# Later slots for transfers, affine maps and softmax steps in a two-layer graph attention kernel

## Chip, cores and metric

The kernel runs on one core of one Trainium2 chip. The metric is the device time of one execution in microseconds; smaller is better. All arithmetic is in fp32.

## What is computed

The input is 128 graphs of 64 nodes with 768 features, and an adjacency matrix for each. After a layer norm with relu, two attention layers follow, and the result is added to the input:

```python
h = jnp.maximum(_layernorm(x, axis=-1), 0.0)
for l in range(2):
    m_left = jnp.einsum('bsh,oh->bso', h, W_left[l])
    m_right = jnp.einsum('bsh,oh->bso', h, W_right[l])
    u_left = jnp.einsum('bih,bjh->bij', h, m_left) / temper
    u_right = jnp.einsum('bih,bjh->bij', h, m_right) / temper
    u = u_left * adj_tri + u_left * diag_mask + u_right * jnp.swapaxes(adj_tri, 1, 2)
    delta_exp_u = jnp.exp(u) * adj
    attention = delta_exp_u / (jnp.sum(delta_exp_u, axis=2, keepdims=True) + 1e-10)
    h_lin = jnp.einsum('bsh,oh->bso', h, W_lin[l]) + b_lin[l]
    ctx = jnp.matmul(attention, h_lin)
    h = jax.nn.relu(_layer_norm(ctx, ln_a[l], ln_b[l]))
return x + h
```

## The kernel before

The 8192 tokens are cut into 16 blocks of 512 tokens (8 graphs each). A block stands in SBUF transposed, features on partitions, in one of four tiles `ht`. Each layer has two passes over all blocks, and DRAM holds what goes from one to the next.

**Pass one** (`pass_one`, L463) takes two blocks at a time; I call that a *set*, `U` = 0 to 7. `project` (L546) multiplies both blocks by the left (`k` = 0) and the right weights (`k` = 1). It does not form the 36 chunk products of 256 x 256 that this would take, but 29 products of sums of weight chunks with sums of token chunks (`PRODUCTS`, L129); each product's PSUM bank is then added, with a sign, to several chunks of the result tiles `m`, one tile per block, two tiles in all. For each of the 29 products and each `k` there are four matmuls (L559) into one PSUM bank, named X, Y, Z, V or aux, and then `read` (L307): the first time a chunk of `m` is written, ScalarE copies (L316); every later time, VectorE adds (L234). A first read happens only in products 0 to 11. Some products accumulate onto the bank of the product before them (product 3 onto product 2's), and then their matmuls wait for that bank's reads. The sums of token chunks (`X_OPS`, tiles `ts`) are made on GpSimd (also L234). The weight sums come from DRAM, where they were stored earlier, through a ring of eight tiles `wp` that is filled seven products ahead (`stream`, L210).

When a set's matmuls are done, `scores` (L488) multiplies `m` with the block's tokens: 192 matmuls of 32 x 95 for each block (L500), into the bank aux0. Before, both blocks' scores stand in one piece behind product 0 of the next set. Then comes the softmax of each block, a generator of eight steps (`chain`, L504): mask on GpSimd (L508), multiplication by the mask on VectorE (L514), exponential on ScalarE (L520), sums and division on VectorE, a transpose (L532), and eight stores of the attention (L537). Meanwhile the next two blocks are made ready: their rows are loaded (L381), in layer 0 normalised (L422, L426, L427), transposed on VectorE (L448), stored to DRAM in transposed form (L444) and loaded again as a block (L386). In layer 1 ScalarE then applies the layer norm's weights and the relu to the loaded block, six instructions called the *affine map* (L393).

The first set of layer 0 (`first`, L588) also normalises and turns its own two blocks on TensorE (`turn`, L648; statistics L635, copies L667), makes the weight sums on VectorE (negations on ScalarE, L199), and stores them (L207) for the later sets. Weight chunks there share tiles `ht2`, `ht3` and `wp` with what comes later. The two blocks themselves are stored, too (L704).

**Pass two** (`pass_two`, L826) multiplies each block by the linear weights in 15 products (`linear`, L1029; matmuls L1043, banks preset with the bias, L822), applies the attention (L851, L874) and normalises. During pass two of layer 0 the weight sums of layer 1 are made on GpSimd (`two_aside`, L1128: raw weights are loaded at L1133, then `weight_op`, then stored).

**What sets the order.** All transfers are issued by SP's queue, in the order of the program; one that has to wait holds those behind it. On every engine, instructions run in the order written. That order is written out with *slots*: in `project` each pair (product `i`, `k`) has two, after its first two matmuls and after its reads, so that a set has 116 slots, four for each product. `put(slot, f)` plans a piece of work for a slot, `put_all` a list of them at successive slots; `run` does what is planned for the slot, or else takes the next entry from the list `idle` (an entry `None` leaves a slot empty). In a set of layer 1, `block(n, slot)` at slots 14 and 62 plans, for the block, four transposes at every second slot, the store, the next rows and the load directly after them, the affine map eight slots on, and the softmax of an older block in eight successive slots.

## Time and profile before

| | |
|---|---|
| two runs | 2976.84 and 2993.67 us, median 2985.26 |
| profiled execution | 2991.47 us, of which the span from the first to the last instruction is 2989.7 |
| TensorE busy (matmul) | 2741.9 us, 92% of the span; mean granted clock 0.964 |
| VectorE / ScalarE / GpSimd busy | 1483.1 (50%) / 847.2 (28%) / 1333.4 us (45%) |
| DMA | 567.79 MB, mean 190 GB/s |
| stages | pass one of layer 0: 0 to 985 us; pass two: to 1488; pass one of layer 1: to 2489; pass two: to 2990 |

PE is TensorE, DVE is VectorE, ACT is ScalarE, POOL is GpSimd, SPq is SP's queue of transfers. A group such as `m<-m,aux` says what is written and read, by the names of tiles. The granted clock is the share of full speed that TensorE gets. In the waits, "A <- B: total, times, longest" says that A stood idle until B was done; "issue" means that nothing which the profile shows held it. A waiting instruction on one engine is often put down to an engine that itself waits, so a wait is followed back until something works.

### The profile page before, as it was taken

What the parts mean: (1) busy time and instruction counts of PE and PEld (TensorE: products, weight loads), DVE (VectorE), ACT (ScalarE), POOL (GpSimd) and SP (SyncE); (2) the same over time, 40 slices, a digit from 0 to 9 for tenths busy, and PEclk for the clock granted to TensorE, in tenths of its full rate; (3) what the DMA queues carried; (4) which work ended last, traced back from release to release, by engine and by line L of the source; (5) the groups of instructions that cost most, each with busy time, mean ns of one, the idle gap of its engine ahead of it and who ended that gap; (6) DMA issues with size and microseconds to landing.
All of it is one profiled execution on the core that took longest, in us unless ns stands there. A gap on an engine that the chain in (4) does not pass through costs nothing.

```text
span 2989.7 us, 47185 instructions
## 1 busy us (share of the span) xinstructions
PE 2741.9 (92%) x18514; PEld 2336.0 (78%) x18514; DVE 1483.1 (50%) x2469; ACT 847.2 (28%) x1635; POOL 1333.4 (45%) x1036
## 2 busy tenths in 40 slices
PE   7699999999999899999889889898898998999998
PEld 6588888888878788888678778787787877888886
DVE  5545546547447333333334434344353474666667
ACT  4221321321210144445521121211212111544443
POOL 3233333332435385655423234232342343888886
PEclk8899999999999999999999999899999999999999
DMA  7658668567673244455766766557675642555555
GB/s 260 188 191 274 207 191 269 186 216 247 193 259 131 98 160 153 159 174 163 223 215 193 230 199 224 175 189 218 196 236 180 213 151 71 149 170 170 164 173 141
DMA packets 310220, 567.79 MB, mean 190 GB/s; under 512 B 62832, under 2 KB 190064, under 8 KB 301808
## 3 DMA queue, kind: packets, MB, share of 16 engines
q1 hardware_dynamic: 309840, 564.39, 59.8%
q8 instruction: 148, 2.42, 0.3%
q14 instruction: 72, 0.59, 0.1%
q10 hardware_dynamic: 160, 0.39, 0.0%
HBM read 429.40 MB, written 135.27 MB: 189 GB/s over the span
## 4 chain that ended last, share of the span: by engine, by line
PE 75%; DMA 8%; DVE 5%; issue 3%; ACT 2%; SPq 2%; POOL 1%; DVEq 0%; ACTq 0%; POOLq 0%
PE aux L559 14%; PE X L1043 11%; PE Y L559 8%; PE X L559 8%; PE V L559 7%; PE V L1043 7%; PE Z L559 5%; PE Y L1043 5%; PE aux L500 4%; PE Z L1043 4%; DMA wp<-ws 3%; DMA ht<-h 2%; PE aux L851 2%; DVE m L234 2%; DMA room<-z 1%
## 5 line engine op out<-in xcount | busy, mean ns | idle before, releaser
L234 POOL TENSOR_TENSOR ts<-ht 128x512 f32<-128x512 f32 x352 | 476.5, 1359 | 294.1 <-PE aux L559 157.6
L234 POOL TENSOR_TENSOR ts<-ht,ht 128x512 f32<-128x512 f32 x128 | 164.6, 1296 | 936.2 <-PE aux L559 351.5
L559 PE MATMUL aux<-ts,wp 128*128 128x252 f32 (+1 forms) x1872 | 456.7, 389 | 123.0 <-DVE m L234 122.3
L559 PEld LDWEIGHTS aux<-ts,wp 128*128 128x128 f32 x1872 | 364.0, 196 | 181.2 <-DVE m L234 134.6
L234 POOL TENSOR_TENSOR ts<-ht,ts 128x512 f32<-128x512 f32 x192 | 254.4, 1329 | 166.7 <-PE aux L559 94.9
L234 DVE TENSOR_TENSOR m<-m,aux 128x504 f32<-128x504 f32 (+1 forms) x304 | 200.6, 673 | 247.0 <-ACT m L316 126.8
L234 DVE TENSOR_TENSOR m<-m,X 128x512 f32<-128x512 f32 x160 | 105.2, 682 | 400.5 <-ACT m L316 357.5
L1043 PE MATMUL X<-room,ts 128*128 128x256 f32 x1024 | 250.4, 387 | 17.6 <-POOL ts L234 7.5
L559 PE MATMUL Y<-ts,wp 128*128 128x256 f32 x1112 | 263.3, 380 | 1.0 <-DVE m L234 1.0
L1043 PEld LDWEIGHTS X<-room,ts 128*128 128x128 f32 x1024 | 195.0, 193 | 52.0 <-POOL ts L234 12.4
L559 PEld LDWEIGHTS Y<-ts,wp 128*128 128x128 f32 x1112 | 211.9, 191 | 29.6 <-issue 1.4
L393 ACT ACTIVATE ht<-ht,b_col,a_col 128x512 f32<-128x512 f32 x192 | 141.9, 803 | 248.5 <-DMA ht<-h 248.5
L500 PE MATMUL aux<-m,ht 128*32 128x95 f32 x6144 | 147.2, 256 | 45.2 <-issue 45.2
L1043 PE MATMUL Y<-room,ts 128*128 128x256 f32 x768 | 183.2, 380 | 0.0
L500 PEld LDWEIGHTS aux<-m,ht 128*32 128x32 f32 x6144 | 137.3, 116 | 56.6 <-issue 56.5
L234 DVE TENSOR_TENSOR m<-m,Y 128x512 f32<-128x512 f32 x176 | 118.2, 679 | 123.6 <-PE Y L559 108.1
L559 PE MATMUL Z<-ts,wp 128*128 128x256 f32 x736 | 174.3, 380 | 1.6 <-DMA wp<-ws 1.6
L1043 PEld LDWEIGHTS Y<-room,ts 128*128 128x128 f32 x768 | 146.7, 191 | 20.8 <-issue 0.6
L559 PEld LDWEIGHTS Z<-ts,wp 128*128 128x128 f32 x736 | 139.4, 190 | 21.5 <-DMA wp<-ws 3.1
L234 POOL TENSOR_TENSOR ts<-ts,ht 128x512 f32<-128x512 f32 x96 | 122.3, 1274 | 67.6 <-PE V L559 52.5
L234 DVE TENSOR_TENSOR hl<-hl,V 128x512 f32<-128x512 f32 (+1 forms) x136 | 88.9, 654 | 125.7 <-PE V L1043 113.6
L559 PE MATMUL X<-ts,wp 128*128 128x256 f32 x616 | 148.6, 385 | 0.0
(212 smaller groups left out, 4644.9 us busy)
## 6 DMA issues: line engine op xcount, KB each, us to landing
wp<-ws SPq DMA_DIRECT2D x435, 512.0 KB, 6.1
ht<-h SPq DMA_DIRECT2D x62, 1536.0 KB, 8.7
h<-room SPq DMA_DIRECT2D x112, 384.0 KB, 5.4
z<-z SPq DMA_DIRECT2D x128, 192.0 KB, 3.2
xr<-in_x_dram SPq DMA_DIRECT2D x120, 192.0 KB, 3.9
out_dram<-xr SPq DMA_DIRECT2D x120, 192.0 KB, 2.7
ws<-wp SPq DMA_DIRECT2D x84, 256.0 KB, 4.1
room<-in_x_dram SPq DMA_DIRECT2D x112, 192.0 KB, 5.3
```

The costliest lines, as they stand in the source:

```text
L234: (eng.tensor_add if sign == "+" else eng.tensor_sub)(o, a, b)
L393: nc.scalar.activation(ht, ht, AF.Relu, bias=cols[1][:, c:c + 1], scale=cols[0][:, c:c + 1])
L500: nc.tensor.matmul(p[h * S + e:h * S + e + 32, q, e:e + 95], ht[:, c, b * S + e:b * S + e + 32], mb[:, e:e + 95], start=(c == 0), stop=(c ...
L559: nc.tensor.matmul(p[:, g], wk[:, c, g * P:(g + 1) * P], tk[:, c, :].rearrange("p (b s) -> p b s", s=S)[:, :, :ns], start=(new and g == c ...
L851: nc.tensor.matmul(cx[k][i, m, :HH], at[j, q, :], hl[j, q, m * HH:(m + 1) * HH], start=True, stop=True)
L1043: nc.tensor.matmul(p[:, n], b[t][:, c, r * P:(r + 1) * P], w[s][:, c, :], start=(i in FIRST and i not in PRELOAD and n == c == 0), stop=(c ...
```

## The change

It moves work between slots; apart from which tiles hold the last block's adjacency and mask, what is computed and what is transferred stays the same.

- In pass one the two blocks' scores come apart: the first block's behind product 0 of the next set, the second's behind product 2. The second result tile `m` is taken anew behind product 2, and reads into it that are due before are held back.
- For each block, transposes start at slots 6 and 48 (layer 1; 20 and 48 in its first set), 6 and 56 (layer 0), 40 and 77 (first set of all). The store follows four slots after the last one, the next rows one later, the load of the block thirteen slots after the transposes, and the affine map 22 slots after the load.
- The softmax has slots of its own, 20 to 34 and 60 to 74, one step in every second slot.
- In each pass's last set both first blocks of pass two are loaded (slots 12 and 40) and mapped (38 and 66). The softmax of the very last block is run in slots 2 to 9 of pass two; its adjacency and mask are kept in a tile of the weight ring.
- In the first set, the turns of the last four row groups come at slots 8, 12, 19 and 24 instead of 9, 11, 17 and 19, the stores of the two first blocks at 54 and 58 instead of 13 and 21.
- In pass two of layer 0 empty slots are put behind the raw weights' loads and behind each weight operation.

The functions `prepare` and `both_scores` go, and the line numbers fall by 4 to 21: the affine map is L381, ScalarE's first read L304, the scores L483, the block load L374, the row loads L369, the block store L432, the first blocks' store L688, the attention's store L520, the stores of weight sums L195, the stream L198, project's matmuls L538, the exponential L503, and additions L222.

```diff
-    singles = [RING[i][:, n] for i in range(RINGS) for n in range(2)]
+    singles = [RING[(NU * NP + 1 + i) % RINGS][:, n] for i in range(RINGS) for n in range(2)]
...
+            def spare(n):
+                return RING[NU * NP % RINGS][:, n].rearrange("p c (q k s) -> p (c q) k s", k=2, s=S)
             def load_adj(u):
-                ADJ[u] = sp.tile([P, Q, 2, S], F32, name="adj")
+                ADJ[u] = spare(0) if u == NB - 1 else sp.tile([P, Q, 2, S], F32, name="adj")
...
-                    wm = sp.tile([P, Q, 2, S], F32, name="wm", bufs=2)
+                    wm = spare(1) if u == NB - 1 else sp.tile([P, Q, 2, S], F32, name="wm", bufs=2)
...
+            TURNS = {0: 0, 2: 1}
             def project(U, weights, done):
...
-                        if i == 0 and k == 1:
+                        late.append((k, p, ns, what))
+                        if k and i in TURNS:
                             if U:
-                                both_scores(U - 1)
-                            for n in range(2):
-                                M[2 * U + n] = sp.tile([P, C, NBB, 2, S], F32, name="m", bufs=2)
-                        for kk in range(2) if (i, k) == (0, 1) else (k,) if i else ():
-                            p, ns = state[kk]
+                                if i == 0:
+                                    both = aux(0)
+                                scores(2 * U - 2 + TURNS[i], both[:, TURNS[i]])
+                            M[2 * U + TURNS[i]] = sp.tile([P, C, NBB, 2, S], F32, name="m", bufs=2)
+                        now, late = late, []
+                        for kk, p, ns, what in now:
+                            if any(2 * U + int(o, 16) % 4 // 2 not in M for o in what[1::2]):
+                                late.append((kk, p, ns, what))
+                                continue
                             read(p, lambda o: M[2 * U + o % 4 // 2][:, o // 4 * K2:(o // 4 + 1) * K2,
...
-                for n, (s0, s1, s2, s3) in {4: (4, 5, 6, 9), 5: (6, 7, 8, 11), 6: (12, 13, 14, 17),
-                                            7: (14, 15, 16, 19)}.items():
+                for n, (s0, s1, s2, s3) in {4: (3, 4, 5, 8), 5: (6, 7, 8, 12), 6: (13, 14, 15, 19),
+                                            7: (17, 18, 20, 24)}.items():
...
-                for n, slot in ((0, 13), (1, 21)):
+                for n, slot in ((0, 54), (1, 58)):
                     put(slot, lambda n=n: nc.sync.dma_start(KEPT[0][n], hts[n]))
...
-                        todo = prepare(u)
-                        load = todo.pop(-2) if u + 1 < NB else todo.pop()
-                        slot = put_all(slot + 1, todo)
-                        slot = max(slot, (86, 99)[n]) if U == 0 and l == 0 else slot
-                        put(slot - 1, load)
+                        *todo, store = transpose_rows(l, u)
+                        slot = put_all(slot, todo)
+                        put(slot + 4, store)
+                        if u + 1 < NB:
+                            put(slot + 5, lambda: load_rows(l, u + 1))
+                        slot = max(slot + 13, (92, 107)[n]) if U == 0 and l == 0 else slot + 13
+                        put(slot, lambda: load_h(1, l, u))
                         if l:
-                            put_all(slot + 8, affine(1, l, u))
-                        if U:
-                            put_all(slot + 1, softmax(u - 4) + [lambda u=u: load_adj(u - 2)])
-
-                    for n, slot in enumerate((32, 60) if U == 0 and l == 0 else (14, 62)):
-                        put(slot, lambda n=n, slot=slot: block(n, slot))
+                            put_all(slot + 22, affine(1, l, u))
+
+                    if l:
+                        starts = (6 if U else 20, 48)
+                    else:
+                        starts = (6, 56) if U else (40, 77)
+                    for n, slot in enumerate(starts):
+                        put(slot - 1, lambda n=n, slot=slot: block(n, slot))
+                    if U:
+                        for n in range(2):
+                            put_all(20 + 40 * n, softmax(2 * U - 2 + n) + [lambda n=n: load_adj(2 * U + n)], 2)
                     put_token_ops(l, U + 1, "before")
                 else:
-                    put(12, lambda: load_h(2, l, 0))
-                    slot = put_all(30, affine(2, l, 0))
                     for n in range(2):
-                        put_all(14 + 10 * n, softmax(2 * U - 2 + n) + [lambda n=n: load_adj(2 * U + n)])
+                        put(12 + 28 * n, lambda n=n: load_h(2, l, n))
+                        put_all(38 + 28 * n, affine(2, l, n))
+                    for n in range(2):
+                        put_all(14 + 20 * n, softmax(2 * U - 2 + n), 2)
+                    put(32, lambda: load_adj(2 * U))
+                    put(SLOTS - 12, lambda: load_adj(2 * U + 1))
...
-            both_scores(NU - 1)
-            for a, b in zip(softmax(NB - 2), softmax(NB - 1)):
-                a()
-                b()
+            both = aux(0)
+            for n in range(2):
+                scores(NB - 2 + n, both[:, n])
+            for f in softmax(NB - 2):
+                f()
+            put_all(2, softmax(NB - 1))
...
-            if (2, l, 0) not in HT:
-                load_h(2, l, 0)
...
                 if u + 1 < NB:
-                    load_h(2, l, u + 1)
-                    put_all(9 if u else 15, affine(2, l, u + 1))
+                    if u:
+                        load_h(2, l, u + 1)
+                        put_all(9, affine(2, l, u + 1))
...
                 idle.extend([lambda n=n, kind=kind: raw(kind, n) for n in range(9)])
+                idle.extend(none * (12 if kind == "l" else 4))
                 for i in range(NP):
-                    ops = [op for op in W_OPS if op[0] == i]
-                    idle.extend([lambda op=op, kind=kind: weight_op(ss, kind, op, nc.gpsimd) for op in ops])
-                    idle.extend(none * min(len(ops), 1))
+                    for op in W_OPS:
+                        if op[0] == i:
+                            idle.extend([lambda op=op, kind=kind: weight_op(ss, kind, op, nc.gpsimd), None])
+                    if idle[-1] is None:
+                        idle.pop()
                     idle.append(lambda i=i, kind=kind: kept(kind, i))
```

What this does to the order, first on ScalarE in set 3 of layer 1, around products 10 and 11. `m_11643` and `m_11644` (now `m_11545` and `m_11675`) are the result tiles, `ht0` and `ht1` the blocks for the next set. Before:

```order
L316 ACTIVATE m_11643<-V_11706 128x2x4x63
L520 ACTIVATE adj_11101<-adj_11101 128x4x64
L316 ACTIVATE m_11643<-Y_11786 128x2x4x64
L393 ACTIVATE ht0_11746<-ht0_11746,b_col_604,a_col_602 128x512 x2
L316 ACTIVATE m_11643<-aux1_9535 128x2x4x63
L393 ACTIVATE ht0_11746<-ht0_11746,b_col_604,a_col_602 128x512 x4
L316 ACTIVATE m_11643<-X_11695 128x2x4x64
L316 ACTIVATE m_11644<-X_11695 128x2x4x64
L316 ACTIVATE m_11643<-V_11706 128x2x4x63
L316 ACTIVATE m_11644<-V_11706 128x2x4x63
```

After:

```order
L503 ACTIVATE adj_11106<-adj_11106 128x4x64
L304 ACTIVATE m_11545<-Y_11784 128x2x4x64
L304 ACTIVATE m_11545<-aux1_9533 128x2x4x63
L304 ACTIVATE m_11545<-X_11696 128x2x4x64
L304 ACTIVATE m_11675<-X_11696 128x2x4x64
L304 ACTIVATE m_11545<-V_11706 128x2x4x63
L304 ACTIVATE m_11675<-V_11706 128x2x4x63
L381 ACTIVATE ht0_11762<-ht0_11762,b_col_602,a_col_600 128x512 x6
L503 ACTIVATE adj_11305<-adj_11305 128x4x64
L381 ACTIVATE ht1_11969<-ht1_11969,b_col_602,a_col_600 128x512 x6
```

The map of the first block (`ht0`) stood between the first reads of products 10 and 11, and now stands behind the last of them.

Next, TensorE at the begin of the same set, with the scores of the set before (`aux0` is their bank). Before:

```order
L559 MATMUL Y_11441<-ht2_11034,wp7_84 128x256 x4
L559 MATMUL aux1_9535<-ht2_11034,wp7_84 128x252 x4
L500 MATMUL aux0_11450<-m_10931,ht0_10322 32x95 x96
L500 MATMUL aux0_11450<-m_10932,ht1_10550 32x95 x96
L559 MATMUL Z_11648<-ht3_11262,wp0_77 128x256 x4
L559 MATMUL aux1_9535<-ht3_11262,wp0_77 128x252 x4
L559 MATMUL X_11666<-ht2_11034,wp1_78 128x256 x4
L559 MATMUL V_11674<-ht2_11034,wp1_78 128x252 x4
L559 MATMUL X_11666<-ts10_11432,wp2_79 128x256 x4
```

After:

```order
L538 MATMUL Y_11439<-ht2_11050,wp7_84 128x256 x4
L538 MATMUL aux1_9533<-ht2_11050,wp7_84 128x252 x4
L483 MATMUL aux0_11448<-m_10833,ht0_10338 32x95 x96
L538 MATMUL Z_11549<-ht3_11257,wp0_77 128x256 x4
L538 MATMUL aux1_9533<-ht3_11257,wp0_77 128x252 x4
L538 MATMUL X_11564<-ht2_11050,wp1_78 128x256 x4
L538 MATMUL V_11573<-ht2_11050,wp1_78 128x252 x4
L483 MATMUL aux0_11448<-m_10963,ht1_10545 32x95 x96
L538 MATMUL X_11564<-ts10_11430,wp2_79 128x256 x4
L538 MATMUL V_11573<-ts10_11430,wp2_79 128x252 x4
```

Two products now stand between the halves of the scores. On ScalarE, the reads that follow, after:

```order
L304 ACTIVATE m_11545<-Y_11439 128x2x4x64
L304 ACTIVATE m_11545<-aux1_9533 128x2x4x63
L304 ACTIVATE m_11545<-X_11564 128x2x4x64
L304 ACTIVATE m_11675<-Z_11549 128x2x4x64 x2
L304 ACTIVATE m_11675<-aux1_9533 128x2x4x63 x2
L304 ACTIVATE m_11545<-V_11573 128x2x4x63
L304 ACTIVATE m_11675<-X_11564 128x2x4x64
L304 ACTIVATE m_11675<-V_11573 128x2x4x63
```

The four reads of Z and aux1 into `m_11675` stand ahead of the read of V from product 2; before, both result tiles were free from the scores on, which stood ahead of product 1.

Last, SP in the first set of layer 0; `ws0` are the stored weight sums by product, `h0_0` and `h0_1` the two first blocks. Before:

```order
L207 DMA ws0_2_88<-room_85 128x512 x2
L704 DMA h0_0_144<-ht0_315 128x3072
L207 DMA ws0_3_89<-ht3_247 128x512 x2
L207 DMA ws0_4_90<-wp7_84 128x512 x2
L704 DMA h0_1_145<-ht1_316 128x3072
L207 DMA ws0_5_91<-room_85 128x512 x2
L381 DMA room_85<-in_x_dram 32x2x768 x8
L207 DMA ws0_6_92<-wp2_79 128x512
L207 DMA ws0_6_92<-ht3_247 128x512
L322 DMA a_col_602<-in_ln_a_dram 128x6x1
L322 DMA b_col_604<-in_ln_b_dram 128x6x1
```

After:

```order
L195 DMA ws0_2_88<-room_85 128x512 x2
L195 DMA ws0_3_89<-ht3_247 128x512 x2
L195 DMA ws0_4_90<-wp7_84 128x512 x2
L195 DMA ws0_5_91<-room_85 128x512 x2
L369 DMA room_85<-in_x_dram 32x2x768 x8
L195 DMA ws0_6_92<-wp2_79 128x512
L195 DMA ws0_6_92<-ht3_247 128x512
L310 DMA a_col_600<-in_ln_a_dram 128x6x1
L310 DMA b_col_602<-in_ln_b_dram 128x6x1
```

The stores of the two first blocks no longer stand among those of the first six products' weight sums, and the row loads move up behind those. Further down the queue, after, the loads of blocks 2 and 3 (`ht2`, `ht3`):

```order
L195 DMA ws0_24_110<-wp4_81 128x512
L432 DMA h0_3_147<-room_85 192x4x128 x4
L369 DMA room_85<-in_x_dram 32x2x768 x8
L195 DMA ws0_25_111<-wp6_83 128x512
L195 DMA ws0_25_111<-wp2_79 128x512
L198 DMA wp5_82<-ws0_0_86 128x1024
L198 DMA wp6_83<-ws0_1_87 128x1024
L198 DMA wp7_84<-ws0_2_88 128x1024
L195 DMA ws0_26_112<-wp3_80 128x512
L195 DMA ws0_26_112<-wp1_78 128x512
L374 DMA ht3_1025<-h0_3_147 128x3072
```

Block 3's load comes behind the first three transfers of the weight stream (`wp5` to `wp7`); before, it stood ahead of them.

More of the change, by code (lines that the diff above doesn't have):

```diff
@@ L539, in scores @@
                 CHAIN[u] = chain()
[L541 to L544 removed]
+            TURNS = {0: 0, 2: 1}
             def project(U, weights, done):
[L547 removed]
+                bank, seen, late = {}, (set(), set()), []
                 for i, (w, t, at, new, what) in enumerate(PRODUCTS):
[L549 removed]
                     for k in range(2):
```

18 lines of the change are left out of this document (3 added, 15 removed).

## Prediction

> **What bounds the kernel now.** First the stages: columns are length, then busy time and instructions of TensorE, its weight loads, VectorE, ScalarE and GpSimd, the granted clock, the share of the DMA engines and GB/s. The rows are the first product set, one set of layer 0, one of layer 1.
>
> ```profile
> 0.00:172.14 172.14, 125.50 (x563) 106.23 (x563) 96.80 (x165) 52.27 (x98) 57.80 (x52) 0.89 0.73 236
> 517.25:632.98 115.73, 110.55 (x850) 97.14 (x849) 62.38 (x116) 27.16 (x40) 39.70 (x35) 0.99 0.68 220
> 1733.21:1860.51 127.30, 111.02 (x850) 97.05 (x849) 54.18 (x88) 22.77 (x38) 41.52 (x36) 0.95 0.63 201
> ```
>
> TensorE is the bound; no other compute engine is busy for even 60% of a set. So the change can only give back TensorE's idle and half-clock time. A set of layer 1 takes 11.6 us longer than one of layer 0 with the same matmuls. Next, TensorE's own waits (total, times, longest), asked stage by stage: three rows of the first set, two of the rest of layer 0's pass one, two of its pass two, one of layer 1's pass one without its last set, one with it, two of layer 1's pass two.
>
> ```profile
> PE aux L559 <- DVE m L234: 29.0, 4, 18.7
> PE aux L658 <- DVE ht L667: 5.1, 2, 4.2
> PE X L559 <- ACT ht L199: 5.0, 1, 5.0
> ...
> PE aux L500 <- issue: 28.0, 11, 3.9
> PE aux L559 <- DVE m L234: 8.9, 11, 2.6
> ...
> PE X L1043 <- ACT hl L316: 14.2, 2, 11.4
> PE X L1043 <- POOL ts L234: 7.5, 1, 7.5
> ...
> PE aux L559 <- DVE m L234: 92.7, 12, 13.7
> PE aux L500 <- issue: 14.6, 14, 3.4
> PE X L1043 <- ACT X L822: 4.1, 1, 4.1
> PE X L1043 <- ACT hl L316: 2.9, 1, 2.9
> ```
>
> The 92.7 us are the largest piece. The timeline of one of them shows who is really late:
>
> ```profile
> 1763.60 4.63 SPq L444 DMA_DIRECT2D h<-room  x4
> 1770.18 6.93 SPq L381 DMA_DIRECT2D room<-z  x8
> 1777.34 0.34 SPq L386 DMA_DIRECT2D ht<-h  x1
> 1779.79 9.69 SPq L537 DMA_DIRECT2D att<-wm  x8
> 1786.51 1.52 ACT L393 ACTIVATE ht<-ht,b_col,a_col 128x512 f32<-128x512 f32 x2 [16.93 <-DMA ht<-h]
> 1787.93 0.57 ACT L316 ACTIVATE m<-aux 128x504 f32<-128x504 f32 x1
> 1788.53 0.68 DVE L234 TENSOR_TENSOR m<-m,aux 128x504 f32<-128x504 f32 x1 [17.39 <-ACT m L316]
> 1789.27 3.31 PE L559 MATMUL aux<-ts,wp 128*128 128x252 f32 x7 [13.46 <-DVE m L234]
> ```
>
> Read upwards: TensorE waits for a PSUM bank, the bank for an addition, the addition for a first read (m<-aux) that stands on ScalarE behind the affine map of a block still in flight. The load left SP at 1777.34, behind eight row loads, and its data were there 9.2 us later. VectorE and ScalarE are victims; what stands ahead of what on ScalarE is the cause.
>
> **The change, term by term.** A slot is a quarter of a product. Products follow each other every 3.42 us (1746.50 to 1749.92 in a fence below), so a slot is 0.86 us.
>
> *A, affine maps.* Before, a layer-1 set's first block is stored at slot 23, loaded at 24 and mapped at 33 to 38, ahead of ScalarE's first reads of products 10 and 11 (slots 40 to 47). After: store 18, rows 19, load 27, map 49 to 54, behind the last first read. From load to map there are 22 slots instead of 9, 18.9 us. SP has the store (4.6 us), the rows (6.9) and some streams ahead of the load; that reaches about slot 34, and 9.2 us of flight end at slot 44. Were the load later still, ScalarE would next hold up the second softmax's exponential near slot 66, 22 slots on. So I take all seven long waits as gone: of the 92.7 us some 91, since five of the twelve are short. After each, TensorE runs for some us at half clock:
>
> ```profile
> 1789.27:1799.27 10.00, 10.00 (x38) 8.62 (x39) 4.27 (x7) 4.20 (x7) 3.77 (x3) 0.81 0.79 284
> ```
>
> 10 us at 0.81 lose 1.9 us, which I use for each long wait; times seven, 13. **A = 104** (bounds 83, if 3 us of each wait stay, to 110).
>
> *B, scores apart.* The 384 small matmuls of a set's scores now come as 192, two products, 192. Inside them TensorE waits for nothing but its own instructions, 28.0 + 14.6 us. The gaps are longer, and halve the clock, where transfers crowd (a set's begin in layer 0, then in layer 1):
>
> ```profile
> 639.23:649.23 10.00, 8.55 (x224) 8.00 (x224) 0.00 (x0) 1.20 (x3) 4.62 (x4) 0.83 0.37 152
> 1863.00:1873.00 10.00, 8.41 (x284) 7.58 (x276) 0.00 (x0) 1.42 (x3) 0.00 (x0) 1.00 0.06 22
> ```
>
> A set's scores meet about two gaps; if the instructions for the second half arrive during the 6.8 us of the products between, 192 meet one half of the time, one gap per set: half of 42.6 goes, 21. That they do is inferred, not shown. The softmax stores and the adjacency load leave the set's end, so the rest of layer 0's gaps should shrink towards layer 1's: 8 more, and 9 of the 7 x 1.7 us of half clock. Against it stands a new wait. Product 1 now has to wait for the second block's result tile, which is free only after the second scores; its four reads queue on ScalarE ahead of the read of product 2's bank V, into which product 3 accumulates.
>
> ```profile
> 1746.50 1.89 PE L559 MATMUL X<-ht,wp 128*128 128x256 f32 x8
> 1746.70 1.07 ACT L316 ACTIVATE m<-aux 128x504 f32<-128x504 f32 x2 [0.61 <-PE aux L559]
> 1749.92 1.89 PE L559 MATMUL X<-ts,wp 128*128 128x256 f32 x8
> 1750.12 0.59 ACT L316 ACTIVATE m<-V 128x504 f32<-128x504 f32 x1 [1.10 <-PE V L559]
> ```
>
> After the scores: 0.2 to start, two such pairs of 1.07, the read of V, 0.6, and a hand-over, about 3.0 us, against 1.7 us (half a product) of product 3's first matmuls: TensorE stands 1.3 us, in 14 sets 18 us. Behind the waiting V matmul stands all of TensorE's queue. **B = 21 + 8 + 9 - 18 = 20** (bounds -18, only the new wait, to 45).
>
> [...]
>
> *C, softmax steps every second slot instead of every slot.* TensorE's short waits for additions (8.9 in layer 0, about as much in layer 1, the largest in each pass's last set, whose weight sums stay) lose a third. **C = 5** (0 to 10).
>
> *D, first set.* Four long waits: 18.7, 7.5 (the second of the 29.0), 5.0, 4.2.
>
> ```profile
> 131.99 1.95 SPq L207 DMA_DIRECT2D ws<-ht  x2
> 139.24 0.32 SPq L386 DMA_DIRECT2D ht<-h  x1
> 149.64 1.29 DVE L234 TENSOR_TENSOR wp<-room,wp 128x512 f32<-128x512 f32 x2 [19.48 <-DMA ws<-wp]
> 61.57 0.69 DVE L234 TENSOR_TENSOR ht<-ht,wp 128x512 f32<-128x512 f32 x1 [8.31 <-DMA ws<-ht]
> 110.71 0.18 DVE L427 RECIPROCAL rs<-sd 128x4 f32<-128x4 f32 x1 [8.30 <-ACT sd L426]
> ```
>
> The longest: SP stood 5.3 us at the block load until weights in that tile were stored; the weight stores behind it went out late, and VectorE needed their tiles. Seven slots later most of that has landed. The 7.5: row loads held a weight store, and were late themselves behind the store of a first block that waited for its turn; that store now comes at slots 54 and 58. The 4.2 goes with four slots between two turns instead of two, the 5.0 with block 3's statistics at slot 77 instead of 61, behind the negations that TensorE wanted. With 4 x 1.9 that is 43. Two new waits: block 3's rows land about slot 84, behind the statistics that want them (up to 8.3 on VectorE, last row; I take 5), and block 3's load stands behind three streams that wait for product 25, issues near slot 119 and is wanted near 125, with ten slots of flight (I take 5). VectorE, busy 96.8, has less slack: 5. **D = 28** (10 to 43).
>
> *E, pass starts.* Before, both softmaxes run on VectorE ahead of pass two's first addition, and ScalarE's read behind two exponentials: 2.9 us per layer. Now one goes ahead, the other over slots 2 to 9.
>
> ```profile
> 994.54 4.51 DVE L514 TENSOR_TENSOR wm<-aux,wm 32x380 f32<-32x380 f32 x8 [8.45 <-issue]
> 1025.67 1.26 POOL L234 TENSOR_TENSOR wp<-wp 128x512 f32<-128x512 f32 x1 [40.24 <-DMA wp<-in_w_left_dram]
> ```
>
> The weight operations now stand behind GpSimd's token sums, so the 7.5 goes; block 1 is loaded and mapped within pass one, so layer 1's 4.1 goes. With 1.9 for each and less 1.5 per layer for the second softmax between the additions (about a third of the 4.51): layer 0 2.9 + 7.5 + 3.8 - 1.5, layer 1 2.9 + 4.1 + 3.8 - 1.5. **E = 22** (12 to 25). The 11.4 us at the turn of the layers stay; SP's order there is nearly the same.
>
> Sum: 104 + 20 + 5 + 28 + 22 = 179. The profiled execution took 2991.47 us (span 2989.7); less 179 that is 2812. It lay 6.2 above the median of the runs shown, so I forecast **2806 us**.
>
> **Rivals.** *The scores give nothing.* For it: gaps of 3.4 us also in layer 1, where transfers are few. Against: the longer ones come with the crowded transfers. B = -18, the sum 141: 2844.
>
> *The wait moves.* The load is late for its new slot as well, the map holds the exponential, that holds VectorE. For it: ScalarE waited 16.9 us for the load. Against: 22 slots of slack. With half of A left, 2858.
>
> *Transfers bind.* A set moves 127.3 us x 201 GB/s, 25.6 MB; at the 220 GB/s of layer 0 it could not pass below 116 us, where I count on 111: 7 x 5 back, 2841. Against: nothing shows 220 to be a ceiling; the first set ran at 236.
>
> *Slower.* SP takes everything in order, and eight ring tiles let the weight stream run seven products ahead: 7 x 3.42 = 23.9 us; with about 9 of flight, as for the load above, 15 are left. A block's transfers need 4.6 + 6.9 + 0.3 + 9.7 = 21.5 us of SP. If spread out they left the stream unserved for longer than 15, TensorE would stand for the excess at each of 28 blocks. The change is a loss from 21.4 us on (179 / 28 = 6.4 over), and at 24 us it ends at 2806 + 28 x 9 = 3058. For it: SP is held at more places in a set. Against: streams stand between the pieces in the new order, and the softmax stores, the longest piece, now come apart from the rows.
>
> *The change does nothing* would need the maps still ahead of the first reads; the order shows that they aren't.
>
> **How the numbers follow.** Forecast 0.70, no gain from the scores 0.11, transfers bind 0.07, the wait moves 0.07, slower 0.04, nothing 0.01. All lower bounds together make a sum of 87, 2898; all upper ones 233, 2752. They won't fall together, so I take 2765 to 2870, which holds the three milder rivals. Over 2% faster is below 2925.6, about what a measurement of this kernel can tell: the forecast and these three, less some for several at once, 0.91; within 2% 0.05; slower 0.04.
>
> **What would show it.** A: no idle ScalarE at the map before product 12, and sets of layer 1 at 110 to 113 us, as long as layer 0's. B: one gap per set's scores, and about 1.3 us before product 3's V matmul. D: no wait over 8 us in the first set. E: pass two of layer 0 without a wait for GpSimd. Wrong, if sets of layer 1 stay above 118 us, or TensorE waits for wp<-ws more than a few us in all.

## The result, and the profile after

The changed kernel takes **2829.85 us** (two runs, 2829.77 and 2829.93) against 2985.26 before: a ratio of 0.9479, 95% interval 0.9365 to 0.9594. The forecast was 2806, the range 2765 to 2870. The gain is 155 us where 179 were counted, and the table shows that most of the difference sits in one stage, the later sets of layer 0. A set runs here from the first matmul of its scores to that of the next, and pass two of layer 1 to the end of TensorE's last matmul; the two profiled executions are compared.

| stage | before, us | after, us | gained |
|---|---|---|---|
| first set of layer 0 | 172.1 | 149.2 | 23.0 |
| the seven sets behind it | 812.6 | 817.8 | -5.2 |
| pass two of layer 0 and first set of layer 1 | 624.5 | 592.6 | 31.9 |
| the seven sets behind it | 880.0 | 778.5 | 101.5 |
| pass two of layer 1 | 489.4 | 479.1 | 10.4 |

Another execution of the changed kernel (e9 below) has 812.8 in place of 817.8, so the -5.2 is known to some 5 us: layer 0's later sets gained nothing.

The stage view (columns as in the prediction's first fence), of the changed kernel: first set, the same sets of layer 0 and layer 1 as before.

```profile
0.00:149.16 149.16, 124.85 (x563) 106.10 (x563) 100.12 (x174) 52.66 (x98) 43.86 (x40) 0.92 0.77 255
504.78:620.74 115.96, 111.15 (x849) 96.79 (x848) 64.21 (x116) 26.90 (x40) 39.54 (x34) 0.99 0.67 221
1668.49:1779.02 110.53, 108.48 (x850) 95.65 (x849) 55.15 (x89) 22.46 (x38) 40.45 (x34) 1.00 0.72 231
```

Layer 1's set fell from 127.3 to 110.5 us at a full clock, and is now shorter than layer 0's, which did not move. TensorE's waits, first over the span (the head of the answer), then the additions alone, asked for layer 0's later sets and for those of layer 1 without its last:

```profile
PE aux L538 <- DVE m L222: 23.1, 18, 3.2
PE aux L483 <- issue: 20.1, 16, 2.6
PE X L1039 <- ACT hl L304: 11.5, 3, 9.3
PE Y L538 <- DMA wp<-ws: 8.9, 5, 4.2
PE V L538 <- ACT m L304: 8.7, 12, 0.7
PE X L538 <- ACT ht L187: 7.4, 1, 7.4
```

```profile
PE aux L538 <- DVE m L222: 16.8, 13, 2.4
```

```profile
PE aux L538 <- DVE m L222: 0.3, 1, 0.3
```

The 92.7 us for additions in layer 1 are 0.3. In layer 0 the same wait grew, from 8.9 to 16.8. The timeline of one such wait (in the set of layer 0 above), VectorE's rows and then the row of TensorE that waits:

```profile
538.87 0.98 DVE L436 STREAM_TRANSPOSE room<-room 128x768 f32<-128x768 f32 x1
539.77 0.38 DVE L501 TENSOR_TENSOR adj<-wm 128x256 f32<-128x256 f32 x1
540.08 1.83 DVE L436 STREAM_TRANSPOSE room<-room 128x768 f32<-128x768 f32 x2
541.94 0.69 DVE L222 TENSOR_TENSOR m<-m,Z 128x512 f32<-128x512 f32 x1
542.54 0.42 DVE L505 TENSOR_TENSOR adj<-adj 128x256 f32<-128x256 f32 x1
542.99 0.42 DVE L507 TENSOR_REDUCE s<-adj 128x4 f32<-128x256 f32 x1
543.33 0.97 DVE L436 STREAM_TRANSPOSE room<-room 128x768 f32<-128x768 f32 x1
544.22 0.64 DVE L222 TENSOR_TENSOR m<-m,aux 128x504 f32<-128x504 f32 x1
```

```profile
544.92 1.63 PE L538 MATMUL aux<-ht,wp 128*128 128x252 f32 x3 [2.38 <-DVE m L222]
```

VectorE does softmax (L501 to L507) and block transposes (L436) in turn, without a pause, and the addition that empties TensorE's bank comes behind them. In layer 0 a block starts at slot 6 with its statistics and normalisation, so the transposes fall on slots 24 to 30; the softmax was put at 20 to 34. All six sets from the second to the seventh have this wait, 2.25 to 2.39 us long.

The 8.9 us for `wp<-ws`, the weight stream, are 4.2 at the end of the first set and 4.7 in layer 0's later sets, where the kernel before had 0.9.

Next, the load and the map of a layer-1 set (it starts at 1668.49): SP's queue, then ScalarE.

```profile
1693.78 0.37 SPq L374 DMA_DIRECT2D ht<-h  x1
```

```profile
1717.33 1.07 ACT L304 ACTIVATE m<-V 128x504 f32<-128x504 f32 x2 [0.61 <-PE V L538]
1718.28 4.33 ACT L381 ACTIVATE ht<-ht,b_col,a_col 128x512 f32<-128x512 f32 x6
```

The map follows the last first read without a wait, as forecast. But the load leaves 25.3 us after the set's start, where before it left after 44.1 (1777.34 - 1733.21): much earlier than the slot 34 that the prediction counted for it, which comes 37.5 us after the set's start.

### The profile page after: what moved, and what is told of

Read it like the earlier page. It is cut to its first block, busy times and chain, and to the rows that moved or that the text cites. A ratio compares the mean times of both kernels' runs of the same rounds, so it can differ in the third digit from the quotient of the medians.

```text
span 2827.8 us, 47204 instructions
## 1 busy us (share of the span) xinstructions
PE 2720.0 (96%) x18514; PEld 2315.8 (82%) x18514; DVE 1500.9 (53%) x2469; ACT 843.5 (30%) x1635; POOL 1337.4 (47%) x1036
## 3 DMA queue, kind: packets, MB, share of 16 engines
q8 instruction: 148, 2.42, 0.4%
## 4 chain that ended last, share of the span: by engine, by line
PE 77%; DVE 8%; DMA 4%; ACT 4%; SPq 3%; issue 3%; POOL 2%; DVEq 0%; ACTq 0%; POOLq 0%
PE aux L538 14%; PE X L1039 11%; PE Y L538 8%; PE V L1039 8%; PE X L538 7%; PE V L538 7%; PE Y L1039 6%; PE Z L538 5%; PE aux L483 4%; PE Z L1039 4%; DVE m L222 3%; ACT m L304 2%; DMA wp<-ws 2%; PE aux L847 2%; DVE room L436 2%
## 5 line engine op out<-in xcount | busy, mean ns | idle before, releaser
L222 POOL TENSOR_TENSOR ts<-ht 128x512 f32<-128x512 f32 x352 | 479.3, 1367 | 313.9 <-PE aux L538 203.9
L222 POOL TENSOR_TENSOR ts<-ht,ht 128x512 f32<-128x512 f32 x128 | 163.9, 1286 | 713.5 <-PE aux L538 288.1
L538 PE MATMUL aux<-ts,wp 128*128 128x252 f32 (+1 forms) x1872 | 439.9, 378 | 7.2 <-DVE m L222 7.2
L538 PEld LDWEIGHTS aux<-ts,wp 128*128 128x128 f32 x1872 | 356.2, 191 | 55.7 <-DVE m L222 11.2
L222 POOL TENSOR_TENSOR ts<-ht,ts 128x512 f32<-128x512 f32 x192 | 254.5, 1329 | 173.3 <-PE aux L538 81.2
L222 DVE TENSOR_TENSOR m<-m,aux 128x504 f32<-128x504 f32 (+1 forms) x304 | 200.9, 674 | 153.8 <-PE aux L538 132.4
L538 PE MATMUL Y<-ts,wp 128*128 128x256 f32 x1112 | 265.9, 382 | 5.8 <-DMA wp<-ws 4.7
L1039 PE MATMUL X<-room,ts 128*128 128x256 f32 x1024 | 244.2, 380 | 2.3 <-ACT hl L304 2.2
L538 PEld LDWEIGHTS Y<-ts,wp 128*128 128x128 f32 x1112 | 212.1, 191 | 36.9 <-issue 6.0
L222 DVE TENSOR_TENSOR m<-m,X 128x512 f32<-128x512 f32 x160 | 105.0, 681 | 233.8 <-ACT m L304 189.7
L222 DVE TENSOR_TENSOR m<-m,Y 128x512 f32<-128x512 f32 x176 | 119.0, 684 | 141.4 <-PE Y L538 137.2
L304 ACT ACTIVATE m<-Y 128x512 f32<-128x512 f32 x32 | 19.1, 597 | 564.6 <-PE aux L483 523.1
L222 POOL TENSOR_TENSOR ts<-ts,ht 128x512 f32<-128x512 f32 x96 | 123.1, 1282 | 113.8 <-PE V L538 71.0
L538 PE MATMUL Z<-ts,wp 128*128 128x256 f32 x736 | 174.0, 379 | 0.0
L381 ACT ACTIVATE ht<-ht,b_col,a_col 128x512 f32<-128x512 f32 x192 | 141.1, 804 | 107.6 <-DMA ht<-h 107.6
L483 PE MATMUL aux<-m,ht 128*32 128x95 f32 x6144 | 137.8, 246 | 20.1 <-issue 20.1
L538 PEld LDWEIGHTS Z<-ts,wp 128*128 128x128 f32 x736 | 139.7, 190 | 19.1 <-POOL ts L222 0.3
L1005 POOL TENSOR_TENSOR z<-z,b 128x768 f32<-128x768 f32 x62 | 112.7, 1831 | 89.8 <-DVE z L1002 89.8
L538 PE MATMUL V<-ts,wp 128*128 128x252 f32 (+1 forms) x608 | 143.8, 379 | 11.7 <-ACT m L304 8.7
```

The source lines that it names most:

```text
L222: (eng.tensor_add if sign == "+" else eng.tensor_sub)(o, a, b)
L304: nc.scalar.activation(to(o), p, AF.Copy, scale=1.0 if sign == "+" else -1.0)
L381: nc.scalar.activation(ht, ht, AF.Relu, bias=cols[1][:, c:c + 1], scale=cols[0][:, c:c + 1])
L483: nc.tensor.matmul(p[h * S + e:h * S + e + 32, q, e:e + 95], ht[:, c, b * S + e:b * S + e + 32], mb[:, e:e + 95], start=(c == 0), stop=(c ...
L538: nc.tensor.matmul(p[:, g], wk[:, c, g * P:(g + 1) * P], tk[:, c, :].rearrange("p (b s) -> p b s", s=S)[:, :, :ns], start=(new and g == c ...
L1005: nc.gpsimd.tensor_add(zs[k], zs[k], rows["b"])
```

## Experiments

e1 to e4 ran on one chip, e5 to e8 on a second, e9 to e12 on a third. The kernel before took 2988.4, 2988.3 and 2984.7 us there.

**The changed kernel again** (e9).

> The changed kernel itself, without an edit, on the same chip as the three next to it: 2830 us (2826 to 2838). It says how far a median of the other runs may be trusted; a difference under its spread is read from the waits of the profile alone.

2828.26 us (four runs, 2825.2 to 2831.7), ratio 0.9473 (0.9450 to 0.9496). So a difference of some 5 us between the kernels below is not read from the times.

**The map alone** (e1), in the kernel before:

```diff
-                            put_all(slot + 8, affine(1, l, u))
+                            put_all(slot + 26, affine(1, l, u))
```

> The kernel before with one number changed: the affine map of layer 1 starts 26 slots after the block load instead of 8. It then stands behind the last first read, while transposes, store, rows and load stay where they were. Theory 'overlap' (the stall needs both: data that land late and first reads queued behind the map; moving either is enough): the long waits of layer 1 go, 2985 - 104 = 2881 us (2868 to 2900), sets of layer 1 at 112 to 115 us, waits of PE for VectorE's additions in layer 1's pass one under 10 us instead of 92.7. Rival 'arrival' (the change helps because the load leaves SP about 19 us earlier in the set): the load still leaves 44 us after the set's start, and its data come about 4 us after the map's new turn, so ScalarE and what is queued behind it still hold TensorE: half or more of the 92.7 us stays, 2930 to 2985 us.

2908.97 us (two runs, 2904.5 and 2913.5): 79 us gained, between the two theories. The long waits are gone (8.0 us are left for additions in layer 1's pass one), but another wait takes a part of their place. Waits of TensorE in layer 1's pass one, the head of the answer:

```profile
PE Y L559 <- DMA wp<-ws: 23.3, 8, 3.9
PE aux L500 <- issue: 14.5, 13, 3.7
PE aux L559 <- DVE m L234: 8.0, 7, 4.4
```

Neither theory had the 23.3 us. One of 2.2 to 3.9 us stands in each set, and SP's queue ahead of the one that ends at 1996.51 shows why:

```profile
1971.81 4.62 SPq L444 DMA_DIRECT2D h<-room  x4
1976.53 1.85 SPq L210 DMA_DIRECT2D wp<-ws  x1
1978.43 6.72 SPq L381 DMA_DIRECT2D room<-z  x8
1985.24 0.37 SPq L386 DMA_DIRECT2D ht<-h  x1
```

Store, rows and load leave in one row, with a single stream between them. So it seems that the stream caught up while TensorE stood for the map, and is late without that stall; e10 tests it.

**The whole block plan of layer 1** (e10), in the kernel before: the map 22 slots after the load, and the transfers apart as in the change (first set of layer 1: 20 in place of 6). The softmax of layer 1 starts at slots 25 and 73, one earlier than in the kernel before.

```diff
+                        if l:
+                            *todo, store = transpose_rows(l, u)
+                            slot = put_all(slot, todo)
+                            put(slot + 4, store)
+                            if u + 1 < NB:
+                                put(slot + 5, lambda: load_rows(l, u + 1))
+                            put(slot + 13, lambda: load_h(1, l, u))
+                            put_all(slot + 35, affine(1, l, u))
+                            return
...
```

> The kernel before with the block plan of layer 1 alone taken from the change: transposes from slots 6 and 48, store, rows and load apart, map 22 slots after the load. Scores stay in one piece, the softmax at slots 25 and 73, layer 0, first set and pass two as before. Theory 'stream' (with the map moved alone, 23.3 us of waits for wp<-ws appeared in layer 1, since store, rows, load and softmax stores leave SP in one row and hold the weight stream; apart they don't): waits for wp<-ws in layer 1 under 5 us, sets of 111 to 113 us, 2881 us (2872 to 2892), all of term A. Rival: the softmax stores, still in one row with little else, hold the stream as long: 2900 to 2915 us, as with the map alone.

2870.11 us (2867.9 to 2872.0), 114.5 gained. TensorE's waits for wp<-ws in layer 1 are 0.4 us, and a set looks like this (119.04 us and a clock of 0.97 in e1):

```profile
2028.40:2138.80 110.40, 108.38 (x849) 95.94 (x848) 55.84 (x90) 22.77 (x38) 40.41 (x34) 1.00 0.71 228
```

Theory 'stream' stands, with a little more gained than its range allows. Taken in this order, 79 us of term A come with the map and 35 with the transfers.

**The map back among the first reads** (e2), in the changed kernel: `slot + 22` is `slot + 8` again.

> The changed kernel with the map back at 8 slots after the load instead of 22, so that it stands among the first reads again; the load keeps its new, earlier place. Theory 'overlap': the load leaves SP 25 us after the set's start, and data are there at 35 us, ahead of the map's turn at about 38 us, so no stall comes back: 2830 to 2840 us, waits of PE for additions in layer 1's pass one under 10 us. Rival 'place' (what the prediction worked out for term A: it is the order on ScalarE that stalls TensorE): the first reads of products 10 and 11 stand behind the map and the seven stalls return, 2830 + 60 to 104 = 2890 to 2934 us.

2827.71 us (two runs, 2827.6 and 2827.9), no change: 'place' falls, 'overlap' stands. In the set that starts at 1781.89, ScalarE's rows are:

```profile
1822.06 4.33 ACT L381 ACTIVATE ht<-ht,b_col,a_col 128x512 f32<-128x512 f32 x6
1830.15 1.09 ACT L304 ACTIVATE m<-X 128x512 f32<-128x512 f32 x2 [3.77 <-PE X L538]
```

The map stands ahead of the reads of product 10 and costs nothing, since its data had come (no wait ahead of it). So with the new transfers the early load does without the later map; by e1 the late map alone removes the long waits as well. How term A is split between the two depends on which is moved first: behind the transfers, the map's move is worth nothing.

**Scores in one piece** (e3), in the changed kernel: both behind product 0, and both result tiles taken there.

```diff
-                        if k and i in TURNS:
+                        if k and i == 0:
...
-                                scores(2 * U - 2 + TURNS[i], both[:, TURNS[i]])
+                                for n in range(2):
+                                    scores(2 * U - 2 + n, both[:, n])
...
```

> The changed kernel with both blocks' scores in one piece behind product 0, and both result tiles taken there. Theory 'fetch' (TensorE's gaps in the scores are instruction blocks of 256, 128 matmuls with their weight loads, that arrive late; 384 small matmuls in a row meet two, 192 meet one): idle time inside the scores goes from 20 to 40 to 45 us, with 5 to 10 us more at half clock; the 8.7 us of waits before product 3's V matmul go; in all + 20 us, 2850 us (2842 to 2860). Rival 'scores give nothing' (gaps have another cause, and don't depend on how the scores are cut): only the 8.7 us go, 2821 us.

2835.94 us (2828.4 to 2840.4), 6 to 8 above the changed kernel, within its own spread and between the two ranges. The waits are clearer; pass one of layer 0, then of layer 1:

```profile
PE aux L483 <- issue: 21.6, 11, 3.2
```

```profile
PE aux L483 <- issue: 12.6, 14, 3.1
```

34.2 us, where the changed kernel has 11.7 + 6.6 = 18.3 in these stages and the kernel before had 42.6. So splitting saves 15.9, less than 'fetch' said, and the new wait for V takes 8.7 back. The other 8.4 can be put down to calmer transfers only in part: e1 and e10, whose layer 0 is that of the kernel before, have 23.0 and 24.1 us of these gaps there, not 28.0.

**Scores in four pieces** (e5), 96 matmuls each, behind product 0's right half, product 1's left and right, product 2's right:

```diff
-            TURNS = {0: 0, 2: 1}
+            TURNS = {(0, 1): (0, 0), (1, 0): (0, 1), (1, 1): (1, 0), (2, 1): (1, 1)}
...
```

> The changed kernel with each block's scores cut once more: 96 small matmuls each behind the left and right half of products 0 to 2 (0 right, 1 left, 1 right, 2 right). Theory 'fetch': 192 instructions of a piece are fewer than a block of 256, and at least 1.7 us of large matmuls lie between pieces, so idle time inside the scores falls from 20 us to under 6: 2812 us (2805 to 2820). Rival: the distance between pieces is too small for a fetch that transfers hold up, so half of the gaps stay, or the first result tile's reads, held until product 1, cost as much as the gaps: 2822 to 2840 us.

2836.08 us (2833.3 to 2836.8). Its waits:

```profile
PE aux L539 <- ACT m L304: 18.7, 15, 2.0
...
PE V L539 <- ACT m L304: 10.3, 14, 0.8
...
PE aux L483 <- issue: 3.3, 6, 0.9
```

The gaps in the scores go from 20.1 to 3.3 us, as 'fetch' says; the rival is right about the price, 18.7 us for the first tile's held reads.

That the gaps go with fetches is also to be seen in the instruction queue. Of the kernel before, TensorE in the scores of a layer-1 set (matmuls in a row are merged), then one gap of layer 0, and the instruction queue (q8) in two stretches of that gap, 523.0 to 524.5 and 524.5 to 525.5:

```profile
1733.21 5.41 PE L500 MATMUL aux<-m,ht 128*32 128x95 f32 x251
1739.21 2.82 PE L500 MATMUL aux<-m,ht 128*32 128x95 f32 x128 [0.58 <-issue]
1742.68 0.36 PE L500 MATMUL aux<-m,ht 128*32 128x95 f32 x5 [0.65 <-issue]
```

```profile
526.95 3.37 PE L500 MATMUL aux<-m,ht 128*32 128x95 f32 x80 [3.93 <-issue]
```

```profile
q1 hardware_dynamic: 176, 0.62, 101.0%
```

```profile
q1 hardware_dynamic: 107, 0.41, 101.5%
q8 instruction: 1, 0.02, 5.5%
```

128 matmuls with their 128 weight loads lie between two gaps, here and in the 11 other scores of the kernel before that have two gaps over 0.25 us. In the first 1.5 of the 3.93 us the data queue takes 101.0% of the DMA engines and no instruction packet comes, then one; 1.5 us after its end TensorE goes on. All 28 gaps over 0.25 us of the kernel before and all 15 of the changed one have such a packet, which ends 1.2 to 1.5 us before TensorE goes on.

**Layer 0's first softmax 13 slots later** (e4), in the changed kernel:

```diff
-                            put_all(20 + 40 * n, softmax(2 * U - 2 + n) + [lambda n=n: load_adj(2 * U + n)], 2)
+                            put_all((20 if l else 33) if n == 0 else 60, softmax(2 * U - 2 + n) + [lambda n=n: load_adj(2 * U + n)], 2)
```

> The changed kernel with the first softmax of each layer-0 set at slots 33 to 47 instead of 20 to 34; layer 1 is as it was. Theory 'crowding' (in layer 0 the softmax steps now fall on the slots of the block's transposes, 24 to 30, and VectorE gets behind with the additions that TensorE waits for): the six waits of 2.3 us per set go, and half of the half-clock time behind them, 14 + 7 = 21 us: 2809 us (2803 to 2815), layer-0 sets at 112 to 114 us instead of 116 to 120. Rival 'the wait moves' (VectorE has the same work, and gets behind at another product): 2825 to 2835 us.

**2797.18 us** (2793.0 to 2798.9), ratio 0.9352 (0.9329 to 0.9376): 33 us below the changed kernel, more than expected. TensorE's waits for additions at aux fall to 0.7 us in layer 0's sets, no other wait grows there, and the seven sets take 784.0 us. Of the 33.8 us that these sets gain, 16.1 are the additions' and 4.7 the weight stream's, which went too; the time at half clock falls from 27.3 to 10.2 us, worth 8.5. 'Crowding' stands, 'the wait moves' falls.

**Bank V read first** (e11), in the changed kernel:

```diff
-                        for kk, p, ns, what in now:
+                        for kk, pp, nn, ww in now[::-1] if (i, k) == (2, 1) else now:
...
```

> The changed kernel with the reads behind product 2 in the opposite order: bank V, into which product 3 accumulates, is read ahead of the four held reads of product 1; every bank goes to its own chunks. Theory 'queue': TensorE's waits for ScalarE before product 3's V matmul, 8.7 us in 12, go and no other wait grows by as much: 2821 us (2815 to 2826). Rival: the held reads come later, and a later product waits for them instead: 2828 to 2838 us.

2817.13 us (2812.3 to 2821.6), 11 below the control on the same chip; the wait of V for ScalarE is 0.4 us in all. Theory 'queue' stands. An earlier form (e6) gave 2812.88 us, but there one variable served two loops, and product 2's V bank went into two chunks of the other block's tile in place of its own; its time says nothing of this question.

> The changed kernel with the reads behind product 2 in the opposite order: bank V, into which product 3 accumulates, is read ahead of the four held reads of product 1. Theory 'queue' (TensorE's wait before product 3's V matmul is the read of V standing behind the held reads on ScalarE): the 8.7 us in 12 waits go, 2821 us (2818 to 2824). Rival: the held reads come later and a later product waits for them instead: 2828 to 2835 us.

**The first set's old turns and stores** (e7): slots 9, 11, 17, 19 and 13, 21 again.

> The changed kernel with the first set's four last turns and the two stores of the first blocks back at their old slots (9, 11, 17, 19 and 13, 21). Theory (term D as worked out: these stores hold SP's queue in front of weight stores and rows): waits of 7.5 and some of the 4.2 us for a turn return with 2 x 1.7 us at half clock, 2830 + 12 = 2842 us (2836 to 2850). Rival: the first set's gain comes from the later block transfers alone (slots 40, 77, 92, 109): 2826 to 2833 us.

2837.12 us (2832.7 to 2841.2), the first set 156.7 us in place of 149.2. Waits of this kernel's first set:

```profile
PE aux L538 <- DVE m L222: 8.5, 3, 6.9
PE X L538 <- ACT ht L187: 7.3, 1, 7.3
PE aux L642 <- DVE ht L651: 5.0, 2, 4.2
```

The 7.5 and the 4.2 of before return as 6.9 and 4.2, and the theory's range holds. The 4.2 has no gain behind it, though: in the changed kernel a turn waits 4.0 us for its normalisation on ScalarE instead. So these slots give 7.5 of the first set's 23 us, and the rest comes from the later block transfers or the later block work, which were not tried apart.

**No empty slots behind the raw loads** (e8), in pass two of layer 0:

```diff
-                idle.extend(none * (12 if kind == "l" else 4))
```

> The changed kernel without the empty slots behind the raw weights' loads in pass two of layer 0 (12 and 4 of them). Theory (term E: the first weight operation on GpSimd waits for its raw weights, and token sums that TensorE needs stand behind it): the wait of 7.5 us with 1.7 us at half clock returns, 2839 us (2836 to 2842). Rival: with block 1 loaded within pass one, the token sums are ahead anyway: 2828 to 2832 us.

2825.91 us (2823.3 to 2830.6): the theory falls. Of 7.5 us only 3.1 return. GpSimd's rows, of the kernel before and then of this one, with TensorE's wait last:

```profile
1025.67 1.26 POOL L234 TENSOR_TENSOR wp<-wp 128x512 f32<-128x512 f32 x1 [40.24 <-DMA wp<-in_w_left_dram]
1031.57 2.48 POOL L234 TENSOR_TENSOR ts<-ht 128x512 f32<-128x512 f32 x2
```

```profile
993.80 1.27 POOL L222 TENSOR_TENSOR wp<-wp 128x512 f32<-128x512 f32 x1 [32.97 <-DMA wp<-in_w_left_dram]
997.98 2.48 POOL L222 TENSOR_TENSOR ts<-ht 128x512 f32<-128x512 f32 x2
999.30 1.99 PE L1039 MATMUL X<-room,ts 128*128 128x256 f32 x8 [3.09 <-POOL ts L222]
```

The token sums (`ts`) that TensorE waits for still stand behind weight operations, so the rival's reason fails as well. Two things make the rest. The first weight operation starts 2.4 us before TensorE comes to want the sums (996.2), where before it started 0.3 us after (1025.3). And two weight operations stand ahead of the sums, not four, since the empty slots behind each operation are still there; that makes 4.2 us in place of 5.9. These were read from the two traces, not tried apart.

**e4 and e11 together** (e12).

> The changed kernel with the first softmax of each layer-0 set at slots 33 to 47 and bank V read first, together. If the two waits are independent: 2797 - 9 = 2788 us (2780 to 2794). If the additions of layer 0 take up what V's earlier read frees: 2797 us or more.

**2782.21 us** (2780.3 to 2785.0), ratio 0.932 (0.9298 to 0.9341), below both kernels and within the range for independent waits. One of its layer-1 sets:

```profile
1518.83:1626.83 108.00, 108.00 (x849) 95.80 (x848) 55.20 (x89) 22.56 (x38) 40.40 (x34) 1.00 0.73 237
```

No idle time at all in this profile: 108.0 us is what the matmuls of a set take.

## Why the prediction was right, and where it was off

The direction, the largest term and the range held. By the stages the sum came out 17 us short (161.6 in place of 179), and that it came so near is in part luck: term A was some 10 us too small, term C more than 20 too large.

- **A, 104 forecast, 114.5 by e10**, over its upper bound of 110. The order on ScalarE was read rightly, and the stall needed it. But it was named as the cause, and by e2 the new transfers remove the stall with the map where it was: late data were the other half. "SP has the store, the rows and some streams ahead of the load; that reaches about slot 34" was wrong: SP runs ahead of the slots (in the set that starts at 1668.49 the load left at 25.3 us, where slot 34 comes at 37.5), and in e2's set the data were there before the old map's turn.
- **B, 20 forecast, about 16 by waits.** One gap in place of two, an estimate from the gaps of before: 21 forecast, 15.9. Calmer transfers: 8 forecast, at most 8.4, and by e1 and e10 about half of that is the run's own spread, so the agreement is luck. The wait before product 3's V: 1.3 us in 14 sets was forecast, 0.7 us in 12 came, at the place that was named. What half clock it saved can't be told apart.
- **C, +5 forecast, about -20 came** (by the sets B and C together are -5.2 in layer 0 and +1.0 in layer 1, 778.5 against e10's 779.5; less B's 16; the stages of e9 make it some 3 us milder). This is the step that failed: "TensorE's short waits for additions lose a third". Every second slot was taken for less load, without asking what else stands on those slots in layer 0. With the softmax out of the way (e4) the pair gives 812.6 - 784.0 = 28.6 in layer 0: the 25 forecast for both would have fitted that order, not this one.
- **D, 28 forecast, 23.0.** The 18.7 and the 7.5 are gone. The 5.0 before a negation came back as the 7.4 above, and the 4.2 before a turn as 4.0, now for ScalarE. "Block 3's load late" did not come; its mirror image did, the stream of the second set held 4.2 us by the rows.
- **E, 22 forecast, about 26:** 31.9 less what e10 gained in that stage (15.9), and 10.4. The size is about right. "The weight operations now stand behind GpSimd's token sums, so the 7.5 goes": they do, but by e8 their place is worth 3.1.
- The forecast took off 6.2 us, by which the profiled execution of before lay above its median. The changed kernel's profiled execution, 2829.77 us, lies at its median. So compared profile with profile the gain is 6 us larger than by the medians, and these 6 are the rest of the 24 us between forecast and result.

Of the rivals, "transfers bind" falls with sets at 231 and 237 GB/s and 110.5 and 108.0 us. "The wait moves" falls: ScalarE does wait for the second block's load, 12 to 14 us in each set of layer 1 but the last, and TensorE waits for nothing behind it. "The scores give nothing" falls by e3, e5 and the packets. "Slower" has a real mechanism, the 23.3 us in e1; in layer 1 the change spread the transfers enough to avoid it. The prediction's own sign, waits for wp<-ws of more than a few us in all, stands at 8.9 us: in a small way that rival came true, in layer 0 and at the end of the first set. The gaps in the scores cost 45.2 us in the kernel before.

## What to carry to other kernels

When work is moved to other slots, list for each engine what else stands on the new slots, in every stage that uses the plan: one table of slots served layer 1 well and made layer 0 pay. A stall made of late data and a queue behind it can be undone from either end, and removing it shows what had been catching up meanwhile. Before splitting or moving a burst of small matmuls, count instructions, not microseconds (here 128 matmuls and 128 weight loads lay between two gaps), and look which reads the split holds back: in four pieces these took 18.7 us where the gaps gave 16.8.

## What the runs showed of the hardware

The instruction queue (q8) moved 148 packets and 2.42 MB, 16 KB each; its packets took 0.3% of the 16 DMA engines' span in the kernel before, where the data queue's took 59.8%. TensorE ran 18514 matmuls and as many weight loads, 250 for each packet.

In the kernel before a gap was 0.58 to 1.20 us in layer 1's seven later sets, but for one of 3.41, and up to 3.93 in layer 0's. In the gap of 3.41 the packet started 1.1 us after the gap did, and the data queue took 105.1% of the engines until then; in that of 3.93 it was 1.5 us at 101.0%. That full engines held these two packets is inferred, and a gap of 2.83 us (at 875.91) had a packet 0.54 us late with the data queue at 26.8%. For the 13 gaps of 0.58 to 1.20 us the packet had started 1.09 us or more before the gap.

Two waits of 2.38 us in the changed kernel were followed by different clocks, 1.00 and 0.55 in the 3.41 us behind each:

```profile
426.57 1.75 PE L538 MATMUL aux<-ht,wp 128*128 128x252 f32 x7 [2.38 <-DVE m L222]
```

```profile
426.57:429.98 3.41, 3.41 (x16) 3.05 (x17) 2.25 (x6) 0.59 (x1) 0.00 (x0) 1.00 0.03 5
544.92:548.33 3.41, 3.41 (x9) 2.81 (x10) 1.57 (x5) 0.00 (x0) 0.00 (x0) 0.55 0.05 10
```

The second wait is the one at 544.92 above. Half clock (0.50 granted, as from 544.60 to 548.02) came in 27 spells in the kernel before and 15 in the changed one. Each lasted 3.41 us or a multiple, up to 17.07, but for the last spell of each trace, and all spells of a trace begin on one grid of 3.41 us.

The two waits differ in where they fall in this grid. In both traces every stretch of the grid that ran at full clock with 2.02 us of idle TensorE or more was followed by half clock (27 and 15 stretches), and none with 1.98 us or less. The wait at 544.92 lies within one stretch (541.19 to 544.61, 2.07 us idle); the one at 426.57 is shared by two (0.95 and 1.43). A spell of 3.41 us at 0.50 costs 1.7 us, so the prediction's 1.7 and 1.9 us for each wait can only be means.
